# The last mixture of experts of an eight-layer kernel: choosing its experts sequence by sequence inside the attention ahead of it, fetching rows further ahead, and taking three roots by bits

## The chip, the cores and the metric

The kernel runs on one core of one Trainium2 chip. The metric is the device time of one execution in microseconds (us); less is better. A core has TensorE (PE, matrix products, with PEld for its weight loads), VectorE (DVE), ScalarE (ACT), GpSimd (POOL) and SyncE (SP, which issues DMAs). Each has its own in-order queue of instructions, and they wait for each other by semaphores.

## The reference, cut to what matters

Four layers follow each other, each an attention and a feed-forward part (ffn), with a residual and a layer norm after each part. All is float32, for 8 sequences of 256 tokens with 256 features in the kernel's view. Only the last two parts are touched by the change: the differential attention `attn3` just as far as work is slipped between its instructions, and the last ffn, a mixture of experts:

```python
def _L3_ffn_ref(hidden_states, gate, gate_up_proj, down_proj):
    ...
    router_logits = jnp.einsum('TD,DE->TE', x, gate)
    routing_weights = jax.nn.softmax(router_logits.astype(jnp.float32), axis=-1)
    top_k_weights, top_k_indices = jax.lax.top_k(routing_weights, TOP_K)
    top_k_weights = top_k_weights / top_k_weights.sum(axis=-1, keepdims=True)
    ...
    gate_up = jnp.einsum('TD,EDF->TEF', x, gate_up_proj)
    g, u = jnp.split(gate_up, 2, axis=-1)
    gated = u * jax.nn.silu(g)
    next_states = jnp.einsum('TEF,EFD->TED', gated, down_proj)
    next_states = (next_states * router_weights[..., None]).sum(axis=1)
```

There are 32 experts with 96 inner features, and each token uses its best 4. The reference computes every expert for every token. After it, `x = _layernorm(x + ffn(x))` is the output.

## The kernel before, in words

The program is one long instruction stream for each engine. Eight phases (`PHASES`) run one after the other; the changed ones are `attn3` and `ffn3`. In these two the order of the instructions on PE, DVE, ACT and POOL is the order in which the Python code writes them (a manual schedule), while the DMAs on SP are placed by the scheduler of the framework.

*The attention.* `attn3` walks over 48 units, six for each of 8 sequences. Iteration n of its loop does `scores` of unit n (products, then the row maxima by DVE, L659, and the exponentials by ACT, L662), `factors` (L672 is one DVE reciprocal for each unit, a handy clock tick) and `differences` of unit n-1 (L696 on DVE, L701 and L704 on POOL, which make the tile v), `turned` of unit n-2 (v is transposed on PE, L721, and its Exp taken, L723) and `values` of unit n-3 (L739). In between, generators are stepped: `projections` of the next sequence, `ends` (the generator `finish`, seven steps, which ends a sequence: its transposes L756, a product with the output weights L804, residual, layer norm, and at last `transpose_x`, L154, with a copy to xT, L118 or L120), and `others`. The function `step(others)` is called once ahead of `scores`, and `step(others, 2)` ahead of `turned`.

*The sort.* The 8 sequences form two groups of four (`GROUPS`), 8 tiles of 128 tokens each. `ffn3_sort` sorts the tokens of one group by expert. It makes router logits (L1909), softmax numerators (L1914, L1916, Exp L1919), the best experts of each tile (L1924 MAX8, L1925), and then calls `place`: a one-hot (L880), a count and a rank by products with a matrix of ones and a triangular one (L894), running sums over tiles (L897 to L903), the first slot of each expert (L908 to L915), and the slot of each token and choice (L922, L923). `scatter` then writes each token's row to its four slots in a DRAM tensor `rows`, with 32 indirect DMAs issued by POOL (L954). `tile_experts` finds the expert of each tile of slots (L936 to L945). The sort of group 0 is put into `others` when the fourth sequence is finished, so it runs between the units of the attention, its scatter at three DMAs a step (`each=3`). The sort of group 1 runs between the tiles of group 0's experts.

*The experts.* `ffn3_experts` runs over 63 tiles of 128 slots for each group, as a pipeline: `turn` (two transposes of a tile of rows, L1973, and a copy, L1975), `up` (the products with the expert's weights, L1981, Silu L1988, product L1990; a copy on POOL of one number, `beat`, L1993, keeps POOL's queue in step), `turn_back` (L1997, L1999), and `down` (L2003, copy L2011, and after every third tile a DMA to the DRAM tensor `outs`, L2013). In group 0 `down` follows `turn` by eight tiles (`LAG`), in group 1 by four. `fetch` (L1962) asks for three tiles of rows with one DMA on SP:

```python
fetch(0)
fetch(3)
if self.down is None:
    self.down = self.load(act, "f3_down", [96, 32, D], split=8)
```

and `turn(j)` calls `fetch(j + 6)` for every third j. The weights `f3_down` are 3.1 MB in eight DMAs on the same queue (L132). Their buffer and those of `xg` lie where the attention's tiles lay, so the first of these DMAs waits for the end of the attention.

*The combination.* `ffn3_combine` gathers the four results of each token from `outs` (L2048, indirect DMAs on POOL, four for each tile of tokens), adds them up with their weights (L2054, DVE), and after two tiles takes `moments` (L183, L184), whose inverse root is a power on POOL (`rsqrt`, L146 and L147), then `normed` (L190) and the store of the output (L197). Group 0's combination runs beside group 1's experts; group 1's comes last and alone.

Of the kernel before, what the change touches and what calls it, by code (L numbers as in the profile page):

```python
# [18 lines left out]
P = 128  # L19
NB = 8  # L20
# [19 lines left out]
class Model:  # L40


    def __init__(self, ctx, tc, ins, out):
# [23 lines left out]
        self.scattering = False  # L67
# [42 lines left out]
    def after(self, *call):  # L110

        self.left.append(call)

# [62 lines left out]
    def moments(self, r):  # L176
# [8 lines left out]
        self.rsqrt(rstd, mv[:, :, 1], 1.0, LN_EPS)  # L185
# [367 lines left out]
    def attn3(self, w, act, keep, start=False, beside=None):  # L553
# [4 lines left out]

        nc = self.nc
# [189 lines left out]
        def finish(b):  # L749
# [64 lines left out]
            if beside and b == GROUPS[0][1] - 1:  # L814
                others.append(beside(keep))
            yield

        others = []
        projections, ends, done = [], [], []

        def step(queue, n=1):

            while n and queue:
                if next(queue[0], StopIteration) is StopIteration:
                    queue.pop(0)
                else:
                    n -= 1

# [5 lines left out]
        for n in range(len(units) + 3):  # L834
# [11 lines left out]
            step(others)  # L846
# [11 lines left out]
            if not self.scattering:  # L858
                step(others, 2)
# [4 lines left out]
        return ends + others  # L864
# [1033 lines left out]
    def ffn3_sort(self, w, g, act, each=1):  # L1898


# [5 lines left out]
        lg = self.ps("t")[:, : n * 32].rearrange("p (t e) -> p t e", e=32)  # L1906
        for t in range(n):
            for c in range(2):
                nc.tensor.matmul(  # L1909
                    lg[:, t, :], self.xt(first + t // 2, t % 2, c), w["gate"][:, c, :],  # L1910
                    start=(c == 0), stop=(c == 1),
                )
        nm = act.tile([P, n], F32, tag="r_nm", name="r_nm", bufs=1)
        nc.vector.tensor_reduce(nm, lg, AX.X, ALU.max)  # L1914
        pr = act.tile([P, n, 32], F32, tag="r_pr", name="r_pr", bufs=1)
        nc.vector.tensor_tensor(  # L1916
            pr, lg, nm.unsqueeze(2).to_broadcast([P, n, 32]), ALU.subtract
        )
        nc.scalar.activation(pr, pr, AF.Exp)  # L1919
        yield  # L1920
        top = act.tile([P, n, 8], F32, tag="r_top", name="r_top", bufs=1)
        idx = act.tile([P, n, 8], U32, tag="r_idx", name="r_idx", bufs=1)
        for t in range(n):
            nc.vector.max(top[:, t, :], pr[:, t, :])  # L1924
            nc.vector.max_index(idx[:, t, :], top[:, t, :], pr[:, t, :])  # L1925
            if t % 4 == 3 or t == n - 1:
                yield
# [17 lines left out]
        for i, _ in enumerate(rows):  # L1945
            if i % each == each - 1:
                yield
# [345 lines left out]
```

## Time and profile before

| | us |
|---|---|
| median of three runs | 2511.77 |
| their range | 2509.81 to 2514.41 |
| the profiled execution | 2512.97 |
| its span, first to last instruction | 2511.2 |

| engine | busy us | share of the span |
|---|---|---|
| PE | 2192.5 | 87% |
| PEld | 1494.2 | 60% |
| DVE | 1431.1 | 57% |
| ACT | 1047.5 | 42% |
| POOL | 916.9 | 37% |

The mean granted clock of TensorE is 0.949 of full speed. The shares are means over the whole program; each phase has a limit of its own. In the trace the last attention's units run from about 1765 us to 2215 us, group 0's experts to 2351 us, group 1's to 2452 us, and the last combination to the end. A line such as "L1981 PE MATMUL ps_a<-w_f_gup,xTg" names the source line, the engine, the operation, the tile written and the tiles read. In a timeline the bracket at the end tells how long the engine was idle before the instruction and what ended that idle time; "issue" there means that nothing which the profile shows was waited for.

### The profile page before, as it was taken

The numbers are of one execution on the slowest core, as the hardware profiler recorded it, in microseconds if no ns is written. First come the engines' busy times: TensorE is split into PE (matmuls) and PEld (weight loads), VectorE is DVE, ScalarE is ACT, GpSimd is POOL, SyncE is SP. The second block draws the span as 40 slices with busy tenths as digits, with TensorE's granted clock in tenths as the row PEclk, the third lists the DMA queues.
The fourth block names the chain that finished last, engine by engine and source line by source line (L and its number), as shares of the span: only waits on it lengthen the run. The fifth ranks groups of instructions, "written<-read, shape, count | busy, mean of one in ns | idle before, by whom it ended". The sixth has DMA issues, their size and how long they took to land. (4 is left out here: it accounts for less than half of the span.)

```text
span 2511.2 us, 36255 instructions
## 1 busy us (share of the span) xinstructions
PE 2192.5 (87%) x11960; PEld 1494.2 (60%) x12016; DVE 1431.1 (57%) x3593; ACT 1047.5 (42%) x3005; POOL 916.9 (37%) x1725
## 2 busy tenths in 40 slices
PE   7998899999999999999999999998877777678990
PEld 4554697756666666666664465555555554457780
DVE  4556486754544543544465454565888878645463
ACT  1334365453544544544432112221766755644450
POOL 1222443343433323333312321000566557833555
PEclk9999999999999999999999999999999978789995
DMA  5000411100000100000260011002000000145663
GB/s 160 1 1 1 165 44 40 59 5 4 3 3 8 47 1 1 1 1 1 74 206 1 1 51 52 1 0 103 1 2 1 1 1 26 41 125 172 213 212 96
DMA packets 92309, 120.76 MB, mean 48 GB/s; under 512 B 9757, under 2 KB 79582, under 8 KB 91102
## 3 DMA queue, kind: packets, MB, share of 16 engines
q1 hardware_dynamic: 82270, 95.75, 11.8%
q0 software_dynamic: 8192, 21.11, 2.8%
q8 instruction: 100, 1.64, 0.3%
q10 hardware_dynamic: 1664, 1.57, 0.2%
q14 instruction: 83, 0.68, 0.1%
HBM read 67.53 MB, written 50.88 MB: 47 GB/s over the span
## 5 line engine op out<-in xcount | busy, mean ns | idle before, releaser
L1391 POOL TENSOR_SCALAR p<-p,rs 128x128 f32<-128x128 f32 (+1 forms) x256 | 104.2, 425 | 294.7 <-DVE rs L1389 290.4
L1381 ACT ACTIVATE p<-ps_s,nm,rq 128x128 f32<-128x128 f32 (+1 forms) x256 | 128.0, 507 | 152.2 <-DVE nm L1379 152.2
L1309 ACT ACTIVATE sq<-ps_a 128x512 f32<-128x512 f32 x126 | 76.0, 603 | 227.2 <-PE ps_a L1301 226.9
L146 POOL TENSOR_SCALAR rsq<-bnmv 128x2 f32<-128x2 f32 x64 | 13.6, 212 | 377.5 <-DVE bnmv L184 369.9
L662 ACT ACTIVATE e<-ps_a,nm 128x128 f32<-128x128 f32 (+1 forms) x256 | 105.9, 435 | 107.7 <-DVE nm L659 98.4
L1310 DVE TENSOR_REDUCE ssk<-sq 128x4 f32<-128x512 f32 x64 | 43.8, 686 | 172.9 <-ACT sq L1309 172.9
L704 POOL TENSOR_SCALAR v<-e,r,nmd 128x128 f32<-128x128 f32 (+1 forms) x256 | 134.6, 537 | 10.0
L1301 PE MATMUL ps_a<-w_a_wq,xT 128*128 128x512 f32 x256 | 122.3, 600 | 12.4 <-DVE k L1323 9.4
L721 PE MATMUL ps_t<-ident,v 128*128 128x128 f32 x384 | 69.2, 317 | 61.7 <-DVE qT L600 29.4
L1301 PE MATMUL ps_a<-w_a_wv,xT 128*128 128x512 f32 x256 | 120.6, 593 | 1.0 <-ACT q L1334 1.0
L1981 PE MATMUL ps_a<-w_f_gup,xTg 128*128 x504 | 111.5, 345 | 11.4 <-DVE xTg L1975 6.9
L696 DVE SCALAR_TENSOR_TENSOR e<-e,c 128x128 f32<-128x128 f32 (+1 forms) x256 | 105.1, 460 | 25.5 <-POOL c L683 25.3
L1310 DVE TENSOR_REDUCE ssq<-sq 128x4 f32<-128x512 f32 x64 | 43.9, 686 | 129.8 <-ACT sq L1309 129.8
L1301 PE MATMUL ps_a<-w_a_wk,xT 128*128 128x512 f32 x248 | 116.5, 593 | 0.0
L1429 PE MATMUL ps_o<-w_a_wo,attT 128*128 128x256 f32 x512 | 111.8, 379 | 0.0
L662 ACT ACTIVATE e<-ps_s,nm 128x128 f32<-128x128 f32 (+1 forms) x256 | 106.8, 452 | 0.0
L1429 PEld LDWEIGHTS ps_o<-w_a_wo,attT 128*128 128x128 f32 x512 | 96.7, 190 | 12.8
L1163 DVE SCALAR_TENSOR_TENSOR yg<-ps_t,xg,yg 128x128 f32<-128x128 f32 x266 | 93.1, 350 | 12.7 <-PE ps_t L1152 3.9
L1368 PE MATMUL ps_s<-kT,qT 128*128 128x256 f32 (+1 forms) x512 | 100.3, 329 | 0.0
L721 PEld LDWEIGHTS ps_t<-ident,v 128*128 128x128 f32 x384 | 50.2, 163 | 81.4 <-issue 31.4
L1415 PE MATMUL ps_o<-pT,V 128*128 128x256 f32 x256 | 79.5, 392 | 19.2 <-ACT pT L120 19.2
L1981 PEld LDWEIGHTS ps_a<-w_f_gup,xTg 128*128 128x128 f32 x504 | 82.4, 197 | 22.2 <-ACT yg L2011 10.6
(410 smaller groups left out, 6041.7 us busy)
## 6 DMA issues: line engine op xcount, KB each, us to landing
rows<-zero SPq DMA_DIRECT2D x42, 384.0 KB, 4.5
xg<-rows SPq DMA_DIRECT2D x42, 384.0 KB, 5.1
outs<-yg SPq DMA_DIRECT2D x42, 384.0 KB, 3.7
w_f_gup<-in_f_gup SPq DMA_DIRECT2D x8, 768.0 KB, 8.6
w_f_w<-in_f_w SPq DMA_DIRECT2D x8, 512.0 KB, 6.3
w_f_down<-in_f_down SPq DMA_DIRECT2D x8, 384.0 KB, 8.3
w_f_up<-in_f_up SPq DMA_DIRECT2D x5, 512.0 KB, 7.3
lrows<-zero SPq DMA_DIRECT2D x12, 204.0 KB, 5.7
```

What stands on the lines that cost most here:

```text
L662: nc.scalar.activation(e[:, s, j * nk : (j + 1) * nk], sc[s][:, j, :], AF.Exp, bias=nm[:, s, j : j + 1], scale=1.0, accum_out=sums[:, s, j ...
L696: nc.vector.scalar_tensor_tensor(d[:, s, h, :], u.e[:, s, h, 1, :], u.c[:, s, h : h + 1], d[:, s, h, :], ALU.mult, ALU.add,)
L704: nc.gpsimd.tensor_scalar(u.v[:, s, h, :], d[:, s, h, :], u.r[:, s, h, 0:1], nm[:, s, h : h + 1], ALU.mult, ALU.add,)
L721: nc.tensor.transpose(ps[:, s, c, :], x, self.ident)
L1163: nc.vector.scalar_tensor_tensor(acc[j], y, c, acc[j], ALU.mult, ALU.add)
L1301: nc.tensor.matmul(ps, self.xt(u.b, t, c), w[which][:, c, u.cols], start=(c == 0), stop=(c == 1),)
L1310: nc.vector.tensor_reduce(out, sq, AX.X, ALU.add)
L1368: nc.tensor.matmul(sc[:, j, :], u.qT[:, h0 + j, qc * P : (qc + 1) * P], u.kT[:, h0 + j, 0:nk], start=(j == 0), stop=False,)
L1381: nc.scalar.activation(u.p[qc][:, h0 + j, :], sc[:, j, :], AF.Exp, bias=nm[:, j : j + 1], scale=r[:, j : j + 1], accum_out=u.sums[qc][:, h ...
L1391: nc.gpsimd.tensor_scalar(u.p[qc][:, j, :], u.p[qc][:, j, :], ri[:, j : j + 1], 1.0, ALU.mult, ALU.mult,)
L1429: nc.tensor.matmul(y[:, t, :], attTs[b][:, h, t * P : (t + 1) * P], w["wo"][:, h, :], start=(h == 0), stop=(h == 15),)
L1981: nc.tensor.matmul(ps, xT[j][:, c, :], w["gup"][:, bass.ds(er[j], 1), c, :].rearrange("p o f -> p (o f)"), start=(c == 0), stop=(c == 1),)
```

## The change

- `ffn3_sort` is taken apart. `ffn3_choose` does the router, the best four, the one-hot, the counts and the running sums for one sequence (two tiles). It is put into `others` as each sequence's `finish` ends, for the first seven sequences inside the attention or right behind it, for the eighth beside group 0's experts.
- `ffn3_place` then does for a group what remains: first slots, slots, and the list `sends`, a generator of scatters, and the experts of the tiles. For group 0 it is queued behind the fourth sequence's choice; its scatters go out two at a step instead of three. What is left of them when the attention ends is issued before the experts begin.
- The best four are found on the logits; the exponentials come later, in `ffn3_weights`, on 4 numbers for each token instead of 32, for group 0 ahead of its experts in the code, for group 1 ahead of the last combination.
- The loop of the attention calls `step(sends or others)` ahead of `scores` and `step(others)` ahead of `turned`.
- `fetch` runs nine tiles ahead instead of six, and three fetches instead of two stand ahead of the weights down in the code.
- In the last combination the inverse roots of three of four sequences are made on DVE, from a shift of the bits of the number and three Newton steps, instead of POOL's power.

The other users of `place` keep it. The core of the diff:

```diff
+    def rsqrt_bits(self, out, v, eng):
+
+        n = v.shape[1]
+        half = self.small.tile([P, 4], F32, tag="nm", name="rsh")[:, :n].bitcast(I32)
+        self.nc.vector.tensor_scalar(half, v.bitcast(I32), 1, None, ALU.arith_shift_right)
+        self.nc.vector.tensor_scalar(
+            out.bitcast(I32), half, -1.0, float(0x5F3759DF), ALU.mult, ALU.add
+        )
+        t = self.small.tile([P, 4], F32, tag="sm", name="rst")[:, :n]
+        for _ in range(3):
+            eng.tensor_tensor(t, out, out, ALU.mult)
+            eng.tensor_tensor(t, t, v, ALU.mult)
+            eng.tensor_scalar(t, t, -0.5, 1.5, ALU.mult, ALU.add)
+            eng.tensor_tensor(out, out, t, ALU.mult)
...
             self.norm_done(b, last=False)
-            if beside and b == GROUPS[0][1] - 1:
-                others.append(beside(keep))
-            yield
...
+            if beside and b < NB - 1:
+                others.append(self.ffn3_choose(beside, keep, b))
+                if b == GROUPS[0][1] - 1:
+                    others.append(self.ffn3_place(beside, 0, keep, sends, each=2))
+            yield
...
-            step(others)
+            step(sends or others)
             if u:
                 u.scores()
...
-            if not self.scattering:
-                step(others, 2)
+            step(others)
             if at(2):
                 at(2).turned()
...
+    def ffn3_choose(self, w, keep, b):
...
+        ps = self.ps("t")[:, :64].rearrange("p (t e) -> p t e", t=2)
+        for t in range(2):
+            for c in range(2):
+                nc.tensor.matmul(
+                    ps[:, t, :], self.xt(b, t, c), w["gate"][:, c, :],
+                    start=(c == 0), stop=(c == 1),
+                )
+        lg = keep.tile([P, 2, 32], F32, tag="r_lg", name="r_lg", bufs=1)
+        nc.vector.tensor_copy(lg, ps)
+        yield
+        idx = keep.tile([P, 2, 8], U32, tag="r_idx", name="r_idx", bufs=1)
+        for t in range(2):
+            nc.vector.max(top[:, t0 + t, :], lg[:, t, :])
+            nc.vector.max_index(idx[:, t, :], top[:, t0 + t, :], lg[:, t, :])
+        fi = keep.tile([P, 2, 4], F32, tag="r_fi", name="r_fi", bufs=1)
+        nc.vector.tensor_copy(fi, idx[:, :, 0:4])
+        nc.vector.tensor_tensor(
+            one[:, two].rearrange("p t k e -> p (t k) e"),
+            w["iota"][:, 0:32].unsqueeze(1).to_broadcast([P, 8, 32]),
+            fi.rearrange("p t k -> p (t k)").unsqueeze(2).to_broadcast([P, 8, 32]),
+            ALU.is_equal,
+        )
+        yield
+        yield
+
+        ps = self.ps("t")[:, :128].rearrange("p (x t e) -> p x t e", x=2, t=2)
+        for x, m in ((0, self.ones), (1, self.behind)):
+            for k in range(4):
+                nc.tensor.matmul(
+                    ps[:, x], m, one[:, two, k, :],
+                    start=(x == 0 and k == 0), stop=(x == 1 and k == 3),
+                )
+
+        for t in (t0, t0 + 1):
+            if t == 0:
+                nc.vector.tensor_copy(upto[:, t, :], ps[:, 0, 0, :])
+            else:
+                nc.vector.tensor_tensor(
+                    upto[:, t, :], ps[:, 0, t - t0, :], upto[:, t - 1, :], ALU.add
+                )
+        nc.vector.tensor_tensor(slot[:, two], ps[:, 1], upto[:, two], ALU.add)
+        yield
...
+        def send():
+            for i, _ in enumerate(rows):
+                if i % each == each - 1:
+                    yield
...
+    def ffn3_weights(self, g, keep):
...
         nc.vector.tensor_tensor(
+            wt, top[:, :, 0:4], top[:, :, 0:1].to_broadcast([P, n, 4]), ALU.subtract
         )
+        nc.scalar.activation(wt, wt, AF.Exp)
...
             if j % 3 == 0:
-                fetch(j + 6)
+                fetch(j + 9)
...
-        fetch(0)
-        fetch(3)
+        for j in (0, 3, 6):
+            fetch(j)
         if self.down is None:
...
-                m = self.moments(rs[b])
...
+                m = self.moments(rs[b], g == 1 and i < 2 * n - 1)
...
+        def step(j):
+
+            if ends and j % 3 == 2:
+                self.step(ends)
+                if not ends:
+                    others.append(self.ffn3_choose(w, keep, last))
+                    others.append(self.ffn3_place(w, 1, keep, sends))
+            elif others:
+                self.step(others)
+            else:
+                self.step(sends)
+
+        wt = self.ffn3_weights(0, keep)
+        while sends:
+            self.step(sends)
         for j, _ in enumerate(self.ffn3_experts(w, 0, act)):
...
+            step(j)
```

## The prediction

> **What bounds the kernel now.** I read the page first, then a table of busy times by stretch whose edges I took from the timeline (the first L672 of each sequence of the attention, the L1973 turns of the last ffn), then the chain of waits and the timeline inside the stretches that stand out. The diff begins in the last attention, and the order of instructions is the same up to there, so only what follows 1765 us can move. Columns: from:to and length, then busy us of PE, PEld, DVE, ACT, POOL, then the granted clock, DMA share, GB/s.
>
> ```profile
> 1916.77:1970.86 54.09, 42.86 (x360) 29.16 (x360) 45.69 (x104) 37.05 (x146) 33.37 (x81) 0.91 0.00 1
> 1970.86:2024.98 54.12, 44.12 (x360) 30.54 (x360) 45.20 (x102) 37.66 (x147) 33.16 (x81) 0.87 0.01 1
> 2024.98:2098.78 73.80, 54.87 (x401) 38.93 (x401) 58.95 (x164) 37.39 (x147) 36.47 (x84) 0.77 0.01 3
> 2098.78:2155.94 57.16, 40.24 (x346) 28.24 (x347) 44.44 (x99) 37.50 (x147) 48.13 (x95) 0.87 0.12 42
> ...
> 2215.24:2262.49 47.25, 34.01 (x188) 28.52 (x188) 17.12 (x52) 19.03 (x57) 7.62 (x29) 0.89 0.65 176
> 2262.49:2292.92 30.43, 25.23 (x150) 21.22 (x149) 19.09 (x81) 12.28 (x40) 4.82 (x15) 0.94 0.36 109
> 2292.92:2340.75 47.83, 44.86 (x273) 38.70 (x272) 20.86 (x64) 23.11 (x90) 33.20 (x59) 1.00 0.65 218
> 2340.75:2351.82 11.07, 7.27 (x32) 4.86 (x31) 1.19 (x4) 4.37 (x15) 3.06 (x6) 0.88 0.63 215
> 2351.82:2451.93 100.11, 97.66 (x568) 82.76 (x566) 57.73 (x182) 49.14 (x190) 48.22 (x103) 0.98 0.70 211
> 2451.93:2511.20 59.27, 0.00 (x0) 0.00 (x0) 22.24 (x56) 0.00 (x0) 34.80 (x40) 0.53 0.32 95
> ```
>
> The first four rows are one sequence of the attention each, six units. Undisturbed it takes 54.1 us with DVE at 84% and PE at 79%: a loop in which several engines wait for one another, DVE the fullest. The third row holds the sort of group 0: 19.7 us more for 13.5 us more of DVE. The second group's experts run at PE's pace (100.1 us, PE 97.7); the first group's take 136.6 us from 2215.24 to 2351.82 for the same 63 tiles. The last 59 us are POOL's gathers. What the stalls are, from the chain, the waits and the timeline:
>
> ```profile
> 2216.34 7.30 DMA w_f_down<-in_f_down
> 2223.66 12.51 DMA xg<-rows
> ...
> SPq L1962 <- PE ps_o L739: 3.5, 1, 3.5
> ...
> 2045.60 0.43 DVE L1914 TENSOR_REDUCE r_nm<-ps_t 128x8 f32<-128x256 f32 x1 [4.60 <-PE ps_t L1909]
> ...
> 2236.30 0.66 PE L1973 MATMUL ps_t<-ident,xg 128*128 128x128 f32 x2 [6.94 <-DMA xg<-rows]
> ...
> 2350.38 0.65 ACT L2011 COPY yg<-ps_o 128x256 f32<-128x256 f32 x2 [3.91 <-DMA outs<-yg]
> ...
> 2469.14 0.94 POOL L2048 DMA_INDIRECT yk<-outs,r_slots  x1 [0.30 <-issue]
> 2470.16 0.19 POOL L146 TENSOR_SCALAR rsq<-bnmv 128x2 f32<-128x2 f32 x1
> 2470.43 0.72 POOL L147 TENSOR_TENSOR rstd<-rsq,nhalf 128x2 f32<-128x2 f32 x1
> ...
> 2471.34 1.17 POOL L2048 DMA_INDIRECT yk<-outs,r_slots  x1 [0.19 <-issue]
> ```
>
> The third fetch of rows stands behind the 3.1 MB of weights on SP's queue and lands 12.5 us after its issue; PE, out of tiles, waits. The second group's first fetch stands ahead of three writes of outs and waits for the last scattered row, so the copies behind the tail's products wait for a buffer (3.9 us). And a root on POOL stretches the 1.25 us between two gathers to 2.20.
>
> **The change part by part.** The sum is made against the profiled execution, 2512.97 us (span 2511.2 and 1.8 around it), which is 1.2 above the median 2511.77.
>
> *The attention.* Removed: the sort of group 0, 19.7 us, and the 3.1 us by which the next sequence exceeds 54.1 (three row DMAs of about 1.25 us per unit fill POOL to 48 of 57 us). Added: one choice for each of six sequences; the seventh falls to the start of the experts. DVE by rows: copy 0.2, twice MAX8, load and find 0.39, cast 0.15, the one-hot a quarter of 1.23, so about 0.3, three sums 0.6: 2.1 us. PE: 8 router passes where L1909 took 7.0 us for 32 at that clock, 1.8 us, and eight small counts, about 0.8. In the order the router passes stand between the transposes of X and the two transposes of v, wait for the copy of xT, and hold one of two "t" banks, so that the second transpose of v waits for the first one's Exp (0.6 us). At the same place of an undisturbed unit (1983 to 1990 us) scores would come 2.1 to 2.6 us later; DVE does its 1.9 us of MAX8 to one-hot in that wait. The counts stand ahead of the next scores, where DVE idled 1.39 us for PE: about 0.9. So 3.2 us a sequence, 19.2 in all. Bounds: 1.5 (all in DVE's 16% idle time but the excess on PE) and 6 (a quarter of 19.7 and the fixed waits again). Placement: seven small ones 1.55, four products and sums 3.5, the experts of tiles 1.0: 6.1 us of DVE, I take 5.0, as some fits in idle time. Rows at two per unit add 2.5 us to POOL's 5.5 of a 9.0 us unit: hidden, and at most 3 us if not. The weights' Exp uses the table that is loaded. Net 19.2 + 5.0 - 22.8 = +1.4 us.
>
> *The start of the experts.* What the words say is not what the queue does. In the order SP issues two of eight weight DMAs, which still wait for the attention's last L739, then three fetches, then six weights. And of 32 scatters at two per unit, four are left behind POOL's last v (ends 2213.38): issues to about 2217.4, landed 2.6 us later (the gap between row and fetch at 2343.23 and 2345.79), so 2220.0, against 2215.39 now. The first turn comes 3.05 us later, as now: 8 us after the end of the attention instead of 3.2. The choice of the seventh sequence has its router passes in that wait, its DVE part and counts cost about 1.5. Then nothing is missing for nine tiles: turn 0 to 5 took 9.4 us, three more at 1.3, so turn 8 at about 8 + 9.4 + 3.9 + 1.5 = 22.8 us, now 25.2 (2240.38). Will the weights be there? 4.33 MB took from 2215.4 to 2236.2, 208 GB/s; 3.54 MB from 2220.0 is 17.0 us, so 22 us after the end: just in time for the first down, and the fetch of tile 9 at about 24. I take a gain of 2.7, bounds -1 and 6. The 12.5 us hole is not won: the weights need nearly the same time, and the rows now come late.
>
> *The second sort.* It lies in the row of 30.43 us: 12 turns, which cost 19.6 at 1.42 and 0.65 more on every third, so 10.8 us, among them 3.8 of L1909 and two table loads of 1.28. What stays: one choice (8 passes 0.9, counts 0.5, DVE's part about 1.6) and the placement (the 28th to 32nd turns lost 1.8): 4.8. Gain 6.0, bounds 3 and 8.
>
> *The boundary of the groups.* 11.07 us from the last turn to the first one of group 1. The order has the fetch now behind two more writes of outs, so the stall of 3.9 goes, but the last row comes one step later, at the beat of the last tile (3.5 us after its turn): row 3.7, landed 6.3, fetch landed 9.3. Next late is the fetch. Gain 1.8, bounds 0 and 4.
>
> *The roots.* Three leave POOL, the fourth stays. Each cost 0.95 between gathers and 0.23 at the next (1.48): I take 3.2 us of the 3.5. They become 15 small DVE instructions of about 0.2 us (L908 to L910 start 0.21 apart), 3.0 a sequence; DVE then has 4.1 (products), 1.2, 3.0 and 0.8, 9.1 us in the 10.0 us of eight gathers. That is the cover; from 0.26 us apiece it is gone.
> Against this stands a rule of the Trainium skill, "SBUF — State Buffer", Who interferes with whom: DVE and GpSimd share a port pair as an exclusive lock, tensor_scalar can take it, and a DMA issued from POOL then waits for its descriptors. Six of the 15 are such: 6 x 0.15 x 3 = 2.7 us, an estimate from the page and L939 (153 ns); then the roots win 0.5 and the sum is 2.7 us worse. In the trace the gathers keep 1.25 us whether DVE idles (2456 to 2458) or runs products and statistics; only the one beside L190 took 1.17. I go by the trace and keep the rule's end in the range.
>
> The exponentials of the last weights (a table load 1.28, Exp, four small ones) lie ahead of the first gather's landing at 2458.1: nothing; uncovered, about 2 us. Nine tiles ahead instead of six: nothing in the second group, where no turn waits for rows.
>
> Sum: +1.4 - 2.7 - 6.0 - 1.8 - 3.2 = -12.3, so 2500.7 by the profiled execution and 2499.5 by the median. I say 2500.
>
> **The rivals.** *The choice costs more in the attention than the sort did.* One mechanism: the router passes wait for xT ahead of v's transposes, scores and all behind them come late, and DVE (84%) can't catch up. Against it: 32 passes at one place cost, with everything, 19.7 us. Even with today from 5.3 us a choice (12.3 / 6 more), slower by over 0.2% from 6.1; at 6.5 it is 2520. *The start gains nothing and the port locks:* -12.3 + 2.7 + 2.7 = -6.9, about 2505; with a choice at 4.5 us as well it is 2513, no change. For it: the weights and tile 9 arrive within a us or two of their need. *The choices disappear in idle time:* at 1.5 us each 10 us less, 2490.
>
> **How the numbers follow.** A measurement of this kernel can tell about 0.2%, 5.0 us. Main case (2494 to 2506): 0.58; the choices hidden (2486 to 2494): 0.10, both faster. The weak gains: 0.17, taken as the same (2507 to 2517). Choice dearer than the sort: 0.15, slower. The range 2487 to 2514 holds about 0.8.
>
> **What would show it.** In the profile after: sequences with a choice at about 57 us, none at 73.8; the first L1973 turn 7 to 9 us after the last L739 and no hole of 8.4 us behind the sixth; the second sort without table loads; 32 gathers 1.25 apart, no L147 between. Wrong if sequences take 60 us or more, if down's first product waits for weights beyond 26 us after the attention's end, or if the gathers' spacing grows beside the roots.

## The result: 0.3% faster, and where the time came from

The changed kernel took 2505.21 us (median of 7 runs, 2500.41 to 2509.47), the kernel before 2514.18 us (7 runs beside it, 2509.81 to 2515.04). The ratio is 0.9968, with a 95% interval of 0.9956 to 0.9979: 8 us by the ratio, 9.0 between the medians, more than the 5 us that a measurement of this kernel can tell from nothing. A second set of runs on another occasion gave 0.9958 (0.9946 to 0.9971). The forecast was 12.3 us less.

The changed kernel scatters more than the one before, and its time goes with the granted clock: the three shortest of the seven (2500.41 to 2503.22 us) had a mean clock of 0.950 to 0.952, the four longer ones 0.944 to 0.946. The execution that was profiled is the longest of its seven, 2509.47 us (span 2507.8), so that the two profiled executions differ by 3.5 us only. The second profile of the same kernel has a span of 2504.3. Everything below is therefore read by stage, from both, and whole runs are used only where they differ by more than this scatter.

First the table of busy times by stretch of the changed kernel (from:to and length, then busy us of PE, PEld, DVE, ACT, POOL, then the granted clock, DMA share, GB/s). It answers the one shown for the kernel before: the sequences 3 to 6 and the last one of the attention, its end to the first turn of the experts, on to turn 12, to turn 62, the boundary of the groups, group 1, and the tail.

```profile
1923.50:1980.80 57.30, 45.09 (x377) 31.22 (x376) 47.58 (x115) 36.95 (x146) 33.33 (x81) 0.88 0.01 1
1980.80:2039.40 58.60, 46.61 (x378) 32.52 (x376) 47.44 (x115) 37.47 (x147) 33.35 (x81) 0.85 0.00 1
2039.40:2100.00 60.60, 47.14 (x390) 31.77 (x392) 53.86 (x138) 37.16 (x147) 38.72 (x87) 0.86 0.03 10
2100.00:2156.90 56.90, 42.45 (x325) 28.97 (x317) 46.45 (x113) 36.76 (x146) 44.46 (x91) 0.84 0.08 29
2156.90:2217.70 60.80, 45.96 (x326) 28.46 (x325) 41.15 (x100) 33.08 (x117) 47.55 (x97) 0.70 0.08 29
2217.70:2227.30 9.60, 3.03 (x15) 2.52 (x14) 0.92 (x2) 0.58 (x1) 2.23 (x3) 0.50 0.62 188
2227.30:2255.90 28.60, 24.00 (x114) 19.75 (x115) 10.89 (x40) 12.19 (x32) 5.41 (x20) 0.76 0.64 167
2255.90:2338.45 82.55, 76.86 (x472) 66.23 (x471) 42.39 (x138) 38.73 (x150) 37.24 (x79) 1.00 0.58 189
2338.45:2351.40 12.95, 7.08 (x32) 4.42 (x30) 1.19 (x4) 4.74 (x16) 4.53 (x8) 0.95 0.58 194
2351.40:2451.50 100.10, 98.17 (x567) 83.23 (x567) 57.95 (x183) 48.45 (x189) 48.40 (x103) 0.97 0.69 211
2451.50:2507.80 56.30, 0.00 (x0) 0.00 (x0) 31.21 (x104) 1.88 (x3) 31.50 (x34) 0.51 0.34 102
```

The sequence of 73.8 us with the sort in it is gone; instead every sequence with a choice takes 57 to 61 us, where an undisturbed one took 53 to 54. Between the attention's end and the first turn stand 9.6 us in which PE works 3 us at half its clock. From turn 12 on the experts of group 0 run at PE's pace with the full clock (82.5 us).

All stages of all kernels that were run, in us, from one profiled execution each; the attention is counted from the first L701 (L672 before) to the end of its last product, turns are counted from that end:

| kernel | up to the attention | attention | end to turn 0 | end to turn 12 | turn 12 to 62 | boundary | group 1 | tail | span |
|---|---|---|---|---|---|---|---|---|---|
| before | 1765.3 | 449.9 | 3.2 | 33.3 | 92.2 | 11.1 | 99.7 | 59.8 | 2511.2 |
| changed | 1766.1 | 451.6 | 9.5 | 38.2 | 82.5 | 13.0 | 100.0 | 56.3 | 2507.8 |
| changed, again | 1766.3 | 451.6 | 9.2 | 36.2 | 82.5 | 11.2 | 100.1 | 56.4 | 2504.3 |
| roots_only | 1766.9 | 450.0 | 3.2 | 35.0 | 91.7 | 11.2 | 99.1 | 56.3 | 2510.3 |
| rows_only | 1766.8 | 450.0 | 3.3 | 29.9 | 92.0 | 11.4 | 99.4 | 59.7 | 2509.3 |
| tables_before | 1767.6 | 447.0 | 4.6 | 32.4 | 92.5 | 11.5 | 100.1 | 59.9 | 2510.9 |
| rows_earlier | 1764.8 | 448.0 | 3.6 | 29.9 | 84.4 | 10.5 | 99.4 | 56.5 | 2493.4 |
| no_tables | 1767.2 | 451.7 | 9.1 | 37.6 | 83.4 | 11.1 | 99.7 | 56.5 | 2507.1 |
| clean_start | 1769.8 | 451.3 | 3.6 | 33.6 | 83.0 | 11.1 | 99.9 | 56.4 | 2505.1 |
| six_ahead | 1766.4 | 445.5 | 9.0 | 35.2 | 82.6 | 11.1 | 101.0 | 56.3 | 2498.2 |
| choice_twice | 1764.9 | 458.4 | 9.4 | 36.3 | 82.3 | 10.5 | 100.6 | 56.3 | 2509.3 |
| choose_in_experts | 1765.2 | 441.7 | 9.2 | 38.4 | 84.9 | 12.2 | 100.7 | 56.9 | 2500.1 |
| passes_later | 1767.2 | 461.7 | 9.5 | 41.7 | 82.9 | 11.0 | 99.7 | 56.4 | 2520.6 |
| three_together | 1764.6 | 445.1 | 3.3 | 34.4 | 84.3 | 10.6 | 101.2 | 56.4 | 2496.7 |

Read from the rows of the kernel before and of the changed one again, the change is +1.0 ahead of the attention, +1.7 in it, +2.9 at the start of the experts, -9.7 from there to turn 62, +0.1, +0.4, and -3.4 in the tail: -7.0, against the -6.9 of the two spans. Two parts pay, the second sort and the roots; the start loses. In the kernel before, the stretch from turn 12 to turn 62 had this row:

```profile
2248.60:2340.75 92.15, 82.56 (x497) 70.62 (x496) 47.18 (x166) 41.74 (x153) 40.13 (x83) 0.98 0.53 172
```

Of the 9.6 us between it and the row of 82.55 above, 5.7 are less busy time of PE (its clock was 0.98 before and 1.00 after) and 3.9 are less idle time. ACT's two table loads in it (at 2264.49 for L1919 and at 2269.54 for L1988) are gone too.

The start of the experts, from the timeline of the changed kernel (start, us, engine and line, and in brackets what ended the idle time ahead):

```profile
2217.87 0.80 SPq L140 DMA_DIRECT2D w_f_down<-in_f_down  x2
2219.59 0.96 POOL L977 DMA_INDIRECT rows<-X,r_slots  x1 [0.30 <-issue]
2224.22 1.45 SPq L2063 DMA_DIRECT2D xg<-rows  x3
2225.72 4.19 SPq L140 DMA_DIRECT2D w_f_down<-in_f_down  x6
2227.27 1.08 PE L2074 MATMUL ps_t<-ident,xg 128*128 128x128 f32 x4 [5.79 <-issue]
2239.74 1.28 ACT L809 ACT_TABLE_LOAD   x1
2241.28 1.28 ACT L810 ACT_TABLE_LOAD   x1
2242.82 1.28 ACT L2089 ACT_TABLE_LOAD   x1
2244.71 0.45 PE L2098 MATMUL ps_s<-ident,h 128*96 128x128 f32 x1 [2.76 <-DVE h L2091]
```

The last of the four late rows is issued at 2219.59 and lands only at 2224.2; SP's fetches stand behind it, and six of the eight weight transfers behind the fetches. Later ACT loads the tables of Ln, Exp and again Silu for the last root of the attention, 4.4 us with the two short activations between; tiles 6 and 7 wait for their Silu meanwhile, and PE for them. In the kernel before, the same loads stood here:

```profile
2229.71 1.28 ACT L780 ACT_TABLE_LOAD   x1
2231.25 1.28 ACT L781 ACT_TABLE_LOAD   x1
2232.79 1.28 ACT L1988 ACT_TABLE_LOAD   x1
```

PE's wait for rows, which ended at 2236.30, covered them.

At the boundary of the groups the stall of 3.9 us for outs has shrunk to 1.03, and the fetch is what is late, as forecast:

```profile
2342.62 0.98 POOL L977 DMA_INDIRECT rows<-X,r_slots  x1 [0.15 <-issue]
2345.32 0.65 ACT L2112 COPY yg<-ps_o 128x256 f32<-128x256 f32 x2 [1.03 <-DMA outs<-yg]
2348.10 0.89 SPq L2063 DMA_DIRECT2D xg<-rows  x2
2351.41 1.12 PE L2074 MATMUL ps_t<-ident,xg 128*128 128x128 f32 x4 [4.97 <-DMA xg<-rows]
```

In the tail, from the same timeline, a root's twelve Newton steps lie beside the gathers:

```profile
2469.12 0.95 POOL L2149 DMA_INDIRECT yk<-outs,r_slots  x1 [0.30 <-issue]
2469.64 0.42 DVE L196 TENSOR_SCALAR rst<-rst 128x2 f32<-128x2 f32 x1
2470.37 0.95 POOL L2149 DMA_INDIRECT yk<-outs,r_slots  x1 [0.30 <-issue]
2470.68 0.17 DVE L196 TENSOR_SCALAR rst<-rst 128x2 f32<-128x2 f32 x1
```

The gathers start 1.25 us apart as if DVE were idle. The price of the neighbourhood, where there is one, falls on DVE: one of three L196 in each root took 0.42 us in place of 0.17.

### The profile page after: what moved, and what is told of

Its sections match the earlier page's. It is cut to its first block, busy times and chain, and to the rows that moved or that the text cites. A ratio compares the mean times of both kernels' runs of the same rounds, so it can differ in the third digit from the quotient of the medians.

```text
span 2507.8 us, 36476 instructions
## 1 busy us (share of the span) xinstructions
PE 2209.5 (88%) x12064; PEld 1502.2 (60%) x12064; DVE 1442.3 (58%) x3662; ACT 1045.1 (42%) x3004; POOL 913.9 (36%) x1717
## 5 line engine op out<-in xcount | busy, mean ns | idle before, releaser
L154 POOL TENSOR_SCALAR rsq<-bnmv 128x2 f32<-128x2 f32 x61 | 12.9, 212 | 376.4 <-DVE bnmv L207 369.0
L750 PEld LDWEIGHTS ps_t<-ident,v 128*128 128x128 f32 x384 | 51.5, 167 | 71.2 <-POOL nmd L730 25.1
```

Source lines behind the costliest of these rows:

```text
L750: nc.tensor.transpose(ps[:, s, c, :], x, self.ident)
```

## The experiments

### The changed kernel again

No edit.

> The changed kernel once more, for a second trace of it. In the first trace the last scattered row of group 1 landed 7 us after the last turn of group 0 and the boundary took 13.0 us; one packet of that row came alone, two us behind the rest. If that is chance, the boundary here is 10.5 to 11.5 us and the run is shorter by as much; if it is the order of the queue, it is 13 again. The whole: 2500 to 2510 us, 0.997 of before.

Measured: 2501.59 us (2500.61 to 2507.62), 0.9958 of before (0.9946 to 0.9971). The boundary took 11.2 us:

```profile
2340.42 0.98 POOL L977 DMA_INDIRECT rows<-X,r_slots  x1 [0.16 <-issue]
2344.24 0.89 SPq L2063 DMA_DIRECT2D xg<-rows  x2
2347.81 1.11 PE L2074 MATMUL ps_t<-ident,xg 128*128 128x128 f32 x4 [3.27 <-DMA xg<-rows]
```

From the last row's issue to the fetch it is 3.8 us here and 5.5 us in the first trace. The six other kernels below that keep the changed order of sends to group 1 have boundaries of 10.5 to 11.1 us, so the 13.0 of the first trace is chance. In the DMA records of the first trace one packet of the last row starts at 2346.88, 1.5 us behind the others, just as a transfer of 16 KB on the instruction queue ends (2345.19 to 2346.89); in the second trace such a transfer comes only behind the row. That fits a packet held up by the other transfer, but isn't shown. In sum, the change moves the boundary by nothing that can be told.

### The roots alone

In the kernel before, only this:

```diff
-                m = self.moments(rs[b])
+                m = self.moments(rs[b], g == 1 and i < 2 * n - 1)
```

with `moments` and `rsqrt_bits` of the change.

> The kernel before, with the three roots by bits on DVE and nothing else of the change. Theory: POOL's 32 gathers lose the 0.95 and 0.23 us of each power, 42.5 us from first to last become 39.1, and the run is 3.4 us shorter (0.9986). Rival, by the rule on the shared port: gathers beside the roots grow longer and the run gains 0.5 us or less. In the changed kernel's trace the first tensor_scalar beside a gather took 0.42 us in place of 0.17 and the gathers kept 1.25, so that I expect the first.

Measured: 2507.71 us (2501.67 to 2512.03), 0.9977 (0.9968 to 0.9986). The gathers take 39.09 us from first to last, where they took 42.51, and the tail 56.3 in place of 59.8. So the roots are worth 3.4 to 3.5 us; the rest of the 4.8 us between the medians (5.8 by the ratio) isn't in the tail. What POOL waited for over the tail, from its waits (line waited for, us in total, times, longest):

```profile
POOL yk L2068 <- issue: 8.8, 29, 0.3
POOL yk L2068 <- DMA outs<-yg: 5.5, 1, 5.5
POOL rsq L146 <- DVE bnmv L199: 3.6, 1, 3.6
POOL yk L2068 <- DVE rstd L189: 0.6, 2, 0.3
```

Of 32 gathers two waited for a DVE instruction of the root, 0.3 us each, which is no more than the 0.3 us that lies ahead of every gather. The rival by the shared port is refuted for these instructions.

### Rows nine tiles ahead, alone

In the kernel before:

```diff
-                fetch(j + 6)
+                fetch(j + 9)
...
-        fetch(0)
-        fetch(3)
+        for j in (0, 3, 6):
+            fetch(j)
```

> The kernel before, with rows asked for nine tiles ahead and three fetches ahead of the weights, and nothing else of the change. Theory: the hole of 8.4 us ahead of turn 6 goes, but the three table loads (4.3 us of ACT), which lay inside it, and the first product down, which needs the weights, come out: turn 12 is 2 to 4 us earlier, and the run 2 to 4 us (0.9985). Rival: the whole hole is won, 7 us or more (0.997). Third: the weights land as much later as the fetch takes, nothing is won (1.000).

Measured: 2509.48 us (2507.76 to 2512.09), 0.9986 (0.9977 to 0.9994); turn 12 at 29.9 us after the attention's end in place of 33.3. The first of the three is right: the hole of 8.4 us ahead of turn 6 is gone, and 3.4 us of it are won. The waits of PE over this stretch show what took the rest, first the kernel before, then this one:

```profile
PE ps_t L1973 <- DMA xg<-rows: 6.9, 1, 6.9
```

```profile
PE ps_s L1997 <- DVE h L1990: 3.2, 2, 2.8
```

The wait for rows is replaced by one for h, which stands behind the Silu behind the three table loads.

### The last root without tables, in both kernels

In the finish of the last sequence, `b == NB - 1`:

```diff
+            if b == NB - 1:
+                for qc in range(2):
+                    g.tensor_tensor(rr[:, qc, :], ms[:, qc, :], self.nhalf[:, :16], ALU.pow)
+            else:
                 nc.scalar.activation(rr, ms, AF.Ln)
                 nc.scalar.activation(rr, rr, AF.Exp, scale=-0.5)
                 ...
```

In the kernel before:

> The kernel before, with the last root of the attention by two powers on POOL in place of Ln and Exp with their table loads. Theory: there the three loads lie inside the 8.4 us in which PE waits for the rows behind the weights, so turn 8 and the run stay as they are, to 1 us (1.000). If turn 8 is 3 us earlier, the loads were not hidden there, and the change did not uncover them.

Measured: 2512.14 us, 0.9996 (0.9987 to 1.0006): nothing. Turn 8 stands at 24.2 us in place of 25.1. That agrees with the trace above, where the loads lie inside the wait for rows; the powers that stood in for them here were hidden as well.

In the changed kernel:

> The changed kernel, with the inverse root of the last sequence of the attention taken by two powers on POOL in place of Ln and Exp on ACT. Theory: at the start of the experts ACT loads three tables in a row (Ln, Exp, Silu, 1.28 us each) and tiles 7 and 8 wait for its Silu, so taking them away brings turn 8 forward by about 3 us, from 27.2 us after the attention's end to 24, and the run by 3 (2502). Rival: the weights down are what turn 9 and the first product down wait for; then turn 8 comes sooner but turn 12 doesn't, and the run stays within 1 us of the changed kernel.

Measured: 2507.91 us (2499.36 to 2509.34), 0.9974 (0.9963 to 0.9984), no shorter than the changed kernel (2501.59 us beside it). Turn 8 came at 23.1 us in place of 26.2 and 27.2: the tables do hold it. Turn 12 stayed (37.6). I had expected the weights as the next wait; what the timeline shows is the substitute itself:

```profile
2241.12 5.81 POOL L811 TENSOR_TENSOR rr<-ms,nhalf 128x16 f32<-128x16 f32 x2
2246.90 1.19 POOL L821 TENSOR_TENSOR att<-att,rr 128x256 f32<-128x256 f32 x2
```

```profile
PE ps_t L828 <- POOL att L821: 3.7, 1, 3.7
```

The two powers take 2.9 us each, and the transposes of att, which stand in PE's order between the tiles, wait 3.7 us for them. So the run shows that the tables hold turn 8, and doesn't show what a free removal would bring.

### The rows sent earlier

In the changed kernel:

```diff
-                    others.append(self.ffn3_place(beside, 0, keep, sends, each=2))
+                    others.append(self.ffn3_place(beside, 0, keep, sends, each=3))
```

> The changed kernel with three rows of group 0 sent in each unit in place of two, so that none is left behind the attention's last unit. Theory: the first fetch of rows waits for the last of four late rows, which landed at 2224.2, 6.5 us after the attention's end; without them the first turn comes 4 us or less after the end in place of 9.5, and the run gains 3 to 5 us (2501). Rival 1: the weights and the ACT tables set turn 9 anyway: the first turn is early, but turn 12 gains under 1 us. Rival 2: three row DMAs a unit fill POOL in the attention and its sequence takes 3 us more, as before the change; the two cancel.

Measured: 2503.41 us (2495.23 to 2504.93), 0.9961 (0.9948 to 0.9974). In the timeline of its profiled execution nothing is left between the attention's end (2212.8) and the fetches:

```profile
2212.95 1.62 SPq L2063 DMA_DIRECT2D xg<-rows  x3
2214.61 5.16 SPq L140 DMA_DIRECT2D w_f_down<-in_f_down  x8
```

Turn 0 comes at 3.6 us in place of 9.2 and 9.5, turn 12 at 29.9 in place of 36.2 and 38.2: 6 to 8 us of this stage, more than was expected, with the tables still in place. Whether POOL gives 3 us back in the attention, as the second rival said, is open. Sequences 5 and 6 take 58.2 and 58.9 us: together as much as in the changed kernel (60.7 and 56.8), but 2.6 more than in six_ahead below (58.7 and 55.8), whose sequences ahead of them ran at the same clock as here. The medians, 2503.41 here and 2501.59 for the changed kernel beside it, don't show the gain; each scatters over 7 to 10 us, and five runs of each can't settle it. The gain of the stage is shown in one trace; that of the whole is open.

### Six tiles ahead again

In the changed kernel, `fetch(j + 6)` and the first fetches `(0, 3)`.

> The changed kernel, with rows asked for six tiles ahead and two fetches ahead of the weights, as before the change. Theory: with the rows late as they are here, the third fetch behind the weights lands at about 24 us after the attention's end and is needed for turn 6 at 21, so turn 6 waits and turn 12 is 3 to 5 us later than the 36.2 to 38.2 of the changed kernel; the run 3 to 5 us longer (2506). Rival: the weights set turn 9 anyway and the third fetch lands with them; turn 12 is the same to 1 us.

Measured: 2503.22 us (2499.88 to 2505.92), 0.9966 (0.9954 to 0.9978); turn 12 at 35.2 us. The rival is right: in the changed kernel the nine tiles bring nothing. With the two experiments above, turn 12 after the attention's end is:

| | rows in time | four rows late |
|---|---|---|
| six ahead | 33.3 (before), 35.0 (roots_only) | 35.2 |
| nine ahead | 29.9 (rows_only), 29.9 (rows_earlier) | 36.2 and 38.2 (changed) |

The distance is worth 3.4 to 5.1 us if the rows are there. With nine tiles ahead the late rows cost 6.3 to 8.3 us, more than that; with six ahead they cost 1.9 at most. Each is a trace or two.

This run showed a second thing. Its instructions in the attention stand in the same order as those of the changed kernel, and yet its attention took 445.5 us where the other took 451.6 twice. The same table of busy times, sequences 2 to 6, the changed kernel again and then this one:

```profile
1865.50:2157.10 291.60, 227.70 (x1835) 157.12 (x1833) 243.22 (x590) 185.86 (x733) 183.87 (x422) 0.86 0.02 8
```

```profile
1866.10:2151.30 285.20, 221.76 (x1839) 152.41 (x1841) 243.08 (x590) 186.39 (x734) 183.82 (x422) 0.89 0.03 9
```

DVE, ACT and POOL do the same work in the same time; the granted clock is 0.86 in the one and 0.89 in the other. The Trainium skill, "TensorE: Matmul & The Clock Gate", Part 1, says that the clock is full or half, decided over windows of 3.4 us which run freely and don't start with the kernel. The traces agree: the clock's records here are stretches of 3.41 us and multiples of it, at 1.0 and at 0.5. In the fourteen traces the first instruction lies anywhere from 0.19 to 3.20 us behind an edge of these windows, as free windows would have it. But the attention's first L701 (or its counterpart) lies 3.12 to 3.21 us behind an edge in all of them, so where the windows fall at its start isn't what differs. Seven traces have the changed kernel's order in sequences 2 to 4, and they form two groups:

| traces | fourth stretch at half clock begins, us behind the first L701 | sequences 2 to 4, us | their granted clock |
|---|---|---|---|
| changed (twice), no_tables, clean_start | 61.6 or 61.7 | 174.1 to 174.3 | 0.85 or 0.86 |
| six_ahead, rows_earlier, three_together | 68.5 or 68.6 | 170.7 | 0.90 |

An eighth, choose_in_experts, lies between (61.6; 172.0; 0.88). So the same order takes one of several courses, with a time and a clock of its own. What decides at that stretch, and whether a wait lowers the clock or the clock makes the wait, isn't shown.

### A choice made twice

In the changed kernel, for sequences 0 to 2:

```diff
+                if b < 3:
+                    others.append(self.ffn3_choose(beside, keep, b))
```

> The changed kernel, with the choices of the sequences 0, 1 and 2 made twice in a row, to price a choice inside the attention. Forecast of 3.2 us a choice: the attention takes 9.6 us more, spread over three or four sequences. If a sequence with a choice costs what the trace shows (3.2 to 5.2 us above one without), 10 to 15. Rival: the second choice stands where engines idle, under 2 us each, 6 in all; the rest of the excess would then be the halved clock, not the choice.

Measured: 2511.16 us (2508.54 to 2514.66), 0.9996 (0.9987 to 1.0006). The attention takes 458.4 us, 6.8 more: 2.3 us for one more choice. In sequences 2 to 4 alone it is 8.4 us (182.4 against 174.1), so 2.8 for a choice; sequence 5 gives 1.4 back. That is less than the 9.6 us of the forecast and near the rival's 6, though against the shorter course of the same order (445.5, in six_ahead) it would be 12.9. The first choice in a sequence costs 4.3 us by the two main traces (sequences 2 to 4: 58.1, 57.3 and 58.6 against 52.9, 54.1 and 54.1). Over all traces, sequences 2 to 4 take 160.0 to 161.1 us without choices and 170.7 to 174.3 with them: 3.2 to 4.8 us a choice, by the course that the clock takes. What a second choice saves could lie in the waits of the first one's place; the next experiment asks.

### The router passes one place later

In the changed kernel's `ffn3_choose`, for sequences 0 to 5 an empty step ahead of the passes and one more ahead of the counts:

```diff
         top, one, upto, slot = self.choices[g]
+        if b < NB - 2:
+            yield
...
         yield
         yield
+        if b < NB - 2:
+            yield
```

> The changed kernel with the router passes of the choices of sequences 0 to 5 one place later, behind v's transposes and ahead of the next scores, in place of between the transposes of X and of v. Theory of the prediction: the passes wait for the copy of xT and hold a bank that v's second transpose needs, which makes most of the 3.3 to 4.4 us by which a sequence with a choice is longer; behind v's transposes the copy is long done, and a sequence is 1 to 2.5 us shorter, five of them 5 to 12 us, the run as much. Rival: the choice costs its own DVE and PE time wherever it stands (2.3 us, as the doubled choice showed): sequences 57 to 58 us as now, the run within 2 us.

Measured: 2524.78 us (2522.32 to 2525.81), 1.0048 (1.0034 to 1.0062): slower than the kernel before. What PE's router passes and their loads waited for, in the changed kernel again and here:

```profile
  DVE xT L126: 13.9, 6
  ACT xT L128: 9.5, 6
```

```profile
  ACT p L752: 1.0, 3
```

The wait for xT that the prediction named is real, 23.4 us over twelve waits of the two queues (the passes and the loads of their weights wait side by side, so about half of that in time), and it goes. The time doesn't: sequences 2 to 4 take 60.2, 57.1 and 59.3 us in place of 58.1, 57.3 and 58.6, and sequence 5, in which the placement now falls into other units, 67.7 in place of 60.7. Neither the theory nor the rival, which said 2 us at most for the run, holds. The passes' own wait isn't the price of a choice. Where the rest of it goes isn't settled; what is shown is that the same instructions, the passes one step later and the counts two, cost the attention 10 us.

### The choices of group 1 beside the experts

In the changed kernel:

```diff
-            if beside and b < NB - 1:
+            if beside and b < GROUPS[0][1]:
...
+        else:
+            for b in range(GROUPS[1][0], last):
+                others.append(self.ffn3_choose(w, keep, b))
```

> The changed kernel, with the choices of the sequences 4, 5 and 6 made beside group 0's experts and not in the attention. Theory: a choice costs 4 us in the attention and 1.5 to 2.4 us of PE and waits beside the experts; two leave the attention (8 us less before its end), three to five come back (turn 62 later by 4 to 5 us measured from the attention's end), and the last scatter falls up to three turns later, which the boundary pays (up to 3 us): the run is 0 to 3 us shorter than the changed kernel. Rival: beside the experts a choice costs as much as in the attention; the run is 2 to 4 us longer.

Measured: 2502.57 us (2500.03 to 2507.69), 0.9967 (0.9953 to 0.9982). The attention is 9.9 us shorter, sequences 6 and 7 together 110.1 us in place of 117.7; the other 2.3 lie ahead of them, where the order is still the same. By stages 2.2 us come back by turn 12, 2.4 to turn 62, 1.0 at the boundary, 0.6 in group 1 and 0.5 in the tail. The spans differ by 4.2 us (2500.1 and 2504.3), the medians by less than their scatter. So the choices win 7.6 us in the attention and give back 6.7 behind it. That they are dearer in the attention than beside the experts isn't shown.

### Both edits of the start

`each=3` and the powers.

> The changed kernel with both edits of its start: three rows a unit, so that none is late, and the last root of the attention by powers, without table loads. Alone the first brought turn 12 from 36 to 38 us after the attention's end to 29.9, the second nothing, since the weights came last. Theory: once the rows are early, the weights are too, and the tables are what is left (4.4 us ahead of turn 8): turn 12 at 26 to 28 and the run 2 to 4 us below the kernel with early rows alone (2500). Rival: the weights are next in line again; turn 12 at 29 to 30, no gain.

Measured: 2506.0 us (2503.14 to 2508.54), 0.9972 (0.9962 to 0.9982). Turn 8 came at 18.4 us, 3 earlier than with early rows alone, and turn 12 at 33.6, 3.7 later. PE's waits of this stretch:

```profile
PE ps_t L828 <- POOL att L821: 2.2, 1, 2.2
PE ps_o L2108 <- DMA xg<-rows: 1.3, 1, 1.3
```

The powers on POOL are next in line, as in the run without tables, and the first product down waits 1.3 us for a DMA. Neither theory holds: what was put in the tables' place costs more than they did.

### Three edits together

`each=3`, group 1's choices beside the experts, and the last root of the attention by bits on DVE:

```diff
+            if b == NB - 1:
+                v = nc.vector
+                v.tensor_scalar(ms, ms, 1.0 / 16.0, 1e-8, ALU.mult, ALU.add)
+                ...
+                v.tensor_scalar(hi, ms.bitcast(I32), 1, None, ALU.arith_shift_right)
+                v.tensor_scalar(
+                    rr.bitcast(I32), hi, -1.0, float(0x5F3759DF), ALU.mult, ALU.add
+                )
+                for _ in range(3):
+                    ...
```

> The changed kernel with three edits: three rows a unit in the attention, the choices of sequences 4 to 6 beside the experts, and the last root of the attention by bits on DVE (some 15 instructions of 0.2 us, 3 us) in place of Ln and Exp and of the powers, which took 2.9 us each on POOL and became the next wait. By stages: the attention 9.9 us shorter, as where the choices stood beside the experts; the first turn 3.6 to 5 us after the attention's end, turn 8 at 18 to 20 and turn 12 at 26 to 29, in place of 9.3, 26.7 and 37.2; from turn 12 to turn 62 up to 3 us more than 82.5; the boundary 10.5 to 12.5. Together 12 to 18 us below the changed kernel's 2503: 2487 to 2493. Rival: the weights or the table of Exp set turn 12 again, at 30 or more; and POOL with three rows a unit gives 3 us of the attention back: 2494 to 2500.

Measured: 2501.49 us (2498.37 to 2505.74), 0.9959 (0.9945 to 0.9972): better than the kernel before, not to be told from the changed one, and outside the 2487 to 2493 that was expected. Turn 0 came at 3.3 us, but turn 7 at 22.5 where early rows alone had it at 16.9, and turn 12 at 34.4, as the rival said, though not for its reason. DVE stands in the way now, from its timeline:

```profile
2227.79 0.74 DVE L802 TENSOR_REDUCE ms<-asq 128x16 f32<-128x256 f32 x2
2231.66 0.19 DVE L821 TENSOR_TENSOR rr<-rr,rrh 128x32 f32<-128x32 f32 x1
2231.77 0.41 DVE L2091 COPY xTg<-ps_t 128x256 f32<-128x256 f32 x1
2232.11 0.24 DVE L2106 TENSOR_TENSOR h<-sg,ps_a 128x96 f32<-128x96 f32 x1
```

For 4 us, 2227.79 to 2231.77, the copies of a tile and its h stand behind the root. The root has now been tried on ACT (4.4 us of tables), POOL (5.8 us of powers) and DVE (4.0 us with its sums); on each, something of the next tiles waits behind it. No version among these beats the changed kernel by more than the scatter.

## Why the prediction came out right, and where its steps did not

The forecast was 12.3 us less, the medians show 9.0 and 11.4. The stages of the two traces add up to 3.5 and 6.9 only, as both are traces of longer executions. A trace on the attention's shorter course, six_ahead, has a span 13.0 us below that of before. Counted from turn 8, the start was wrong by 4 to 5 us and the boundary by 2 to 4 in one direction, the second sort by 1 to 2 in the other. So the total held in part by luck.

*The attention, forecast +1.4:* +1.7 in both traces. That it agrees so closely is chance, since the same order took 6.1 us less in six_ahead. The price of 3.2 for a choice stands at the low end of what was measured, 3.2 to 4.8, and was 4.3 in the two traces that are compared. Against that, sequences 5 and 6, in which the sort and its rows lay, fell from 131.0 to 117.5 us with two choices, the placement and two rows a unit in them. The mechanism that the 3.2 was built on, the passes' wait for xT, is there (passes_later takes it away) but isn't what sets the price.

*The start of the experts, forecast -2.7 at turn 8:* this step failed. Turn 8 came at 27.2 and 26.2 us after the attention's end, not at 22.8, against 25.1 before: a loss of 1 to 2. (From 25.1 to 22.8 is a gain of 2.3; the forecast took 2.7.) Two terms were wrong. The late rows landed at 2224.2, 6.5 us after the attention's end and not 4.8, since the last one took 4.5 us from its issue where 2.6 was assumed from a place without the weights on the queues; the first turn followed at 9.5 and not at 8. And there was no term for the three table loads: they were in the trace of before, at 2229.7 to 2234.1, inside the hole that the change removes. Taking a hole away uncovers what lay in it. tables_before and no_tables show both halves, nothing won there, 3 to 4 us at turn 8 here.

*The second sort, forecast -6.0, bounds 3 and 8:* counted from turn 8, as the sum was, 100.4 us became 93.5 and 92.4, so 6.9 and 7.9, inside the bounds; from turn 12, where the start's disorder is over, 92.2 became 82.5, 9.7 less. The term was too small. Its reasons are there, no table load between the tiles, and 8 router passes in place of L1909's 32; in the trace PE is busy 76.9 of 82.5 us at full clock. All kernels with the split choice have 82.3 to 84.9 here, all with the sort 91.7 to 92.5. This is the largest gain of the change.

*The boundary, forecast -1.8, bounds 0 and 4:* +0.1 and +1.9, and 0 over all runs. The stall for outs went and the fetch was next late, both as said; the row landed later than the estimate, and the whole gain was used up.

*The roots, forecast -3.2:* -3.4 to -3.5. The rule of the shared port, which would have made it 0.5, is not borne out for these instructions: the gathers kept 1.25 us.

*Nine tiles ahead,* costed at nothing but the start: 3.4 to 5.1 us when the rows are in time (rows_only), nothing with the late rows of the change (six_ahead). The forecast's remark that the hole "is not won" was right for a reason that it had only half: the rows come late, and in the hole stood the tables.

Of what was to be seen: sequences of about 57 us, yes; the first turn 7 to 9 us after the attention's end, nearly, 9.2 and 9.5; no hole behind the sixth turn, right, but 4.4 us between turns 7 and 8; gathers 1.25 apart, yes, but for one of 1.32 behind each root. Of the signs of being wrong, sequence 5, with a placement and a choice in it, took 60.7 us, and the last one 60.8 (59.3 before), just over the 60. The first product down came 29.5 us after the attention's end, but the last weights had landed at 24.0, 2 later than estimated, and it didn't wait for them. The rival of the dearer choice fell: a choice costs 2.3 us or more as a second one and 3.2 to 4.8 by the lengths of the sequences, under the 5.3 at which all would have been lost. Yet passes_later, slower than before by two empty steps, shows how near that case lay.

## What to carry to other kernels

Before counting a hole as won, list what the other engines do inside it: here three table loads sat in a wait of 8 us and came out with it, and each other home for that root made a wait of its own. A transfer issued earlier is worth nothing while its data come late: look at who produces last, and count that producer's landing with the load that will be on the queues. And where the granted clock goes up and down inside a chain of short loops (here at 78% of PE), the same order of instructions can take 6 us more or less in one stage. So compare stages over several traces, at equal clock, before reading a few us as a cause.

## What the hardware showed that was not expected

- The same instruction order took 451.6, 451.6 and 445.5 us in the attention, at granted clocks of 0.86, 0.86 and 0.89 over sequences 2 to 6, with DVE's busy time equal to within 0.5 us. Seven traces of one order part at the same half-clock stretch, some 62 us into the attention.
- Beside a gather that POOL issues, a small tensor_scalar of DVE can take 0.42 us in place of 0.17 (one in each root); the gathers themselves kept their spacing, 1.25 us, but for one of 1.32 behind each root. If this is the shared port, the loser was DVE.
- A power of 128x16 took 2.9 us on POOL, where one of 128x2 takes 0.69 to 0.85.
- A scatter of 128 rows, 128 KB, took 2.4 us from issue to landing in the quiet, 4.0 and 4.5 beside the weight transfers, and 2.4 to 5.6 between the experts' tiles, by the landings on record in the traces of the two kernels.
